# Seven products for the candidate's aggregation side, ScalarE normalisations and a fused last update in a four-layer graph network kernel

## Chip, cores and metric

The kernel runs on one core of a Trainium2 chip. The metric is the device time of one execution in microseconds (us), here the median of three runs. A core has five engines that run side by side, each with its own queue in order: TensorE (PE, matrix products; its weight loads are shown apart as PEld), VectorE (DVE), ScalarE (ACT), GpSimd (POOL), and SyncE (SP), which in this kernel issues nearly all DMAs. Products land in PSUM, eight banks of 128 x 512 f32; everything else lives in SBUF, and data that must change its layout goes through DRAM.

## What is computed

128 graphs of 128 nodes with 256 features pass four layers. Each layer adds its result to its input and normalises over the features:

```
x = layernorm(x + L0(x, adj, a0..a3))          # attention, one score product for each edge kind
x = layernorm(x + L1(x, adj, W_msg, W_upd))    # mean over neighbours
x = layernorm(x + L2(x, adj, weight, w_ih, w_hh, b_ih, b_hh))   # three gated steps
x = layernorm(x + L3(x, adj, W, a))            # attention, elu

# L2, with A = (adj != 0) and h = x; three times:
m    = h @ weight[i];  aggr = A^T m
gi   = aggr @ w_ih.T + b_ih;  gh = h @ w_hh.T + b_hh
r    = sigmoid(i_r + h_r);  z = sigmoid(i_z + h_z)
n    = tanh(i_n + r * h_n)                     # the candidate
h    = (1 - z) * n + z * h
```

All is f32; the neighbour sums of layer 2 are made of three bf16 parts that together hold the f32 value.

## The kernel before

**Tiling.** Four graphs form a group (G = 4, T = 512 nodes), and there are 32 groups (NG). Features lie in KC = 2 blocks of 128. In layer 2 the state is kept turned: two tiles hT of [128 features, 512 nodes]. `turned` and `back` turn a tile by way of DRAM: a 32 x 32 block transpose on DVE, a store, four loads. `turned_quick` does it on PE and is used at the very start and end, where nothing else fills the wait.

**Order.** The program first records every operation of all groups as an `Op` with a due time (`paced` spreads a stage's operations between two times, in units of PERIOD, offset by the group). Then a planner (from line 902 on) walks a model of the five engines: at each point it issues, on the engine that can start first, the ready operation with the earliest due time. The cost functions (lines 244 to 258), LANDING (a DMA's time) and HOP, PE_HOP and SLACK (the step from one engine to another) set when the model holds an operation ready. The outcome is a fixed order for each engine; the chip keeps that order and waits on semaphores. So several groups are always under way at once, in different stages.

**Layer 2, function `step`.** For each of three steps: `aggregate` makes the neighbour sums of both feature blocks (24 bf16 products) and ACT copies them to agT. Every gate needs a product of a 256 x 256 weight block with the 256 x 512 state. `gate` does it with seven products of 128 x 128 by 256 columns in place of eight, on sums and differences of the blocks (`sums` for the data, w_sh and w_sm for the weights). The four output quarters share partial sums: one PSUM bank, `shared`, takes products 1, 6, 7 and 4 one after another, and between them `snapshot` has ACT copy the state of the bank to SBUF. The next product into that bank has to wait for the copy. A second bank, `other`, takes 2, 5 and 3, and DVE adds the two parts. `gate` is used for the hidden side of the candidate (q, seven products), and for r and z (hidden and aggregated side together, fourteen each). The aggregated side of the candidate is made by `direct` (line 667): plain products, two 512-column ones for each of the two blocks, left in PSUM.

```
n1, d1 = candidate(1, direct(w_i, agT, C + 1), t1, q1)
n0, d0 = candidate(0, direct(w_i, agT, C), t0, q0)
```

`candidate` (line 757) forms (r + 1) q on DVE, adds the PSUM sum on DVE, takes tanh on ACT and h - n on POOL. `update` (line 766) makes the new h = n + 0.5 (z + 1)(h - n) on DVE in two instructions, and turns it back to rows (tile hn, through way_h), after which the next step's bf16 parts are split off.

**Between the layers.** Layer 1's result x2 is stored as rows to way_x2, and turned to way_2, from which the first step's h0T is read. Layer 3 (line 811) reads both again: rT from way_2, to which POOL adds hT, and x3 from way_x2, to which DVE adds hn. So rT and x3 hold x2 + h, once turned and once as rows. The products with w3x read rT; the mean is taken out of w3x beforehand, so only 1/sigma (rstd) is needed there.

**Normalisation.** `statistics` makes mean and variance on DVE and the power -1/2 on POOL. `normalise` (line 468) handles even graphs on POOL (on DVE at the start and end, `quick`) and odd graphs on ACT, with nmr = -mean * rstd. There are four normalisations a group.

Of the kernel before, what the change touches and what calls it, by code (L numbers as in the profile page):

```python
# [18 lines left out]
def kernel(  # L19
# [123 lines left out]
    FAST = ("tensor_scalar", "tensor_scalar_add", "tensor_scalar_mul")  # L143

# [10 lines left out]
    class Op:  # L155
        def __init__(self, engine):
            self.engine, self.calls, self.took, self.landing = engine, [], 0.0, 0.0
            self.after, self.bufs, self.waiting = {}, [], 0
            self.ready, self.nominal, self.urgent = 0.0, 0.0, False
            self.waits = self.holds = False  # L160
            self.rush = 0.0

    class Engine:
# [24 lines left out]
        def __getattr__(self, name):  # L188
            def call(*args, **kw):
# [8 lines left out]
                n = 1  # L198
                for v in out + ins:
                    n = max(n, m_of(v))  # L200
                short = self is PE and BF16 in [v.buf.dtype for v in ins]
                op.took += SPLIT if short else self.cost(name, n, "accum_out" in kw)
                op.landing = LANDING if name == "dma_start" else 0.0

                tensors = [v for v in ins if m_of(v) > 4]
                if self is POOL:
                    op.waits, op.holds = True, name == "memset" or len(tensors) > 1
                elif self is DVE and name not in ("transpose", "bn_stats"):
                    op.waits = op.holds = not any(v.buf.pool is psum for v in out + tensors) and (
                        len(tensors) > 1 or (name in FAST and m_of(out[0]) > 4)  # L210
                    )
# [27 lines left out]
    LANDING = 4.2  # L239
    HOP = 0.235  # L240
    PE_HOP = 0.55
    SLACK = 0.873

    def pe_cost(op, n, sums):
        return 0.11 if op == "transpose" else 0.222 if n <= P else 0.003 + n / 599.0

    SPLIT = 0.056

    def dve_cost(op, n, sums):
        return 0.14 + n * (0.00056 if op in FAST else 0.00106)  # L250

    def act_cost(op, n, sums):
        return 0.6 if op == "dma_start" else 0.17 + n * 0.001 + (0.2 if sums else 0.0)

    def pool_cost(op, n, sums):
        return 0.2 + n * 0.00266 if op in FAST else 0.55 if op == "memset" else 1.2 if n < 64 else 0.25 + n * 0.0023
# [5 lines left out]
    SP = Engine("SP", nc.sync, lambda op, n, sums: 0.6)  # L262
# [3 lines left out]
    PERIOD = 82.744  # L266
    SPAN = 2.0
    EAGER, RUSH = 5.34, 0.516
    L0_START, L0_END, L1_START, L1_END, L3_START, L3_END = -2.032, -1.293, -0.75, -0.05, 0.173, 0.919
    H_END, M_START, M_END = 0.179, 0.179, 0.503  # L270

    def paced(start, end, pe_only=False):
# [3 lines left out]
        for op, t in zip(line, took):  # L276
            op.nominal = (start + (end - start) * sofar / total) * PERIOD
            op.urgent = pe_only
            sofar += t
        line.clear()  # L280

# [24 lines left out]
    w_sm = tile_of("w_sm", [P, NL, 3, 2, P])  # L306

    def weights():
# [3 lines left out]
        for src, tag, bufs in ((w_ih, "hT", 6), (w_hh, "rest", 4)):  # L312
# [9 lines left out]
        paced(-2.6, -2.5)  # L322
        for k, a in enumerate((a0, a1, a2, a3)):
            SP.dma_start(out=acol[:, k, :], in_=a.rearrange("(c p) -> p c", p=P))
        paced(-2.2, -2.1)
# [8 lines left out]
        paced(-2.0, -1.5)  # L334
# [22 lines left out]
        for i in range(NL):  # L357
            wT = tile_of("h0T", [P, KC, D], 4)
# [23 lines left out]
        for n in range(NL + 1):  # L382
            by, gates = POOL if n > 1 else DVE, 3 if n == 0 else 2
# [35 lines left out]
        paced(-1.9, -0.2)  # L419


    def turned(src, n, tag):

        way = tile_of(f"way_{tag}", [n, P, P], 8 if tag == "2" else 4, F32, dram)
        for first in range(0, n, G):
            z = tile_of("z", [P, G, P], 4)[:, : min(n, G)]
            DVE.transpose(z, src[:, first : first + G])
            SP.dma_start(out=way[first : first + G].rearrange("n p c -> p n c"), in_=z)
        return way

# [7 lines left out]
    def turned_quick(dst, blocks):  # L438
# [5 lines left out]
        ACT.copy(dst, ps[:, : len(blocks) * P])  # L444
# [10 lines left out]
    def statistics(res, tag):  # L455
# [3 lines left out]
        rstd = tile_of(f"rstd_{tag}", [P, n], 2)  # L459
        for b in range(n):  # L460
# [5 lines left out]
        return mv, rstd  # L466

    def normalise(res, mv, rstd, tag, quick):

        n = res.shape[1]  # L470
        nmr = tile_of(f"nmr_{tag}", [P, n], 2)
        DVE.scalar_tensor_tensor(nmr, mv[:, :, 0], -1.0, rstd, op0=OP.mult, op1=OP.mult)
        for b in range(0, n, 2):
            (DVE if quick else POOL).tensor_scalar(
                res[:, b, :], res[:, b, :], mv[:, b, 0:1], rstd[:, b : b + 1],
                op0=OP.subtract, op1=OP.mult,
            )
        for b in range(1, n, 2):
            ACT.activation(
                res[:, b, :], res[:, b, :], AF.Identity, bias=nmr[:, b : b + 1], scale=rstd[:, b : b + 1]  # L480
            )
# [26 lines left out]
    def loading(g, s):  # L508
# [12 lines left out]
        paced(g - 2.4, g - 2.1)  # L521
        SP.dma_start(out=s.x, in_=x[graphs].rearrange("b n d -> n b d"))
        paced(g - 1.9, g - 1.8)


    def layer0(g, s):
# [51 lines left out]
        normalise(res, *statistics(res, "0"), "0", g == 0)  # L578
# [12 lines left out]
    def layer1(g, s):  # L591
# [32 lines left out]
        normalise(res, *statistics(res, "1"), "1", g == 0)  # L624

        s.way_x2 = tile_of("way_x2", [P, G, D], 4, F32, dram)
        SP.dma_start(out=s.way_x2, in_=res)
        s.hT, s.parts, s.ways = [], [], []
        for c in range(KC):
            t = tile_of("h0T", [P, T], 4)  # L630
# [12 lines left out]
    def gru(g, s):  # L643
# [5 lines left out]
        def step(i, hT, parts):  # L649
# [16 lines left out]

            def direct(w, v, q, ps=None, of=(0, 1), stop=True):

                start = ps is None
                ps = ps or bank("ps" if q >= C else "gate")  # L670
                with PE:
                    for k in of:
                        PE.matmul(
                            ps, w[:, k, q * P : (q + 1) * P], v[k],
                            start=(start and k == of[0]), stop=(stop and k == of[-1]),
                        )
                return ps
# [25 lines left out]
            def gate(tag, q, sources, copied, added, last=None):  # L703
# [14 lines left out]
                def snapshot(quarter):  # L718
                    copied(t[:, quarter], shared[:, :H], quarter // 2)
                    ops[-1].rush = RUSH  # L720
# [36 lines left out]
            def candidate(c, ps, t, q):  # L757
                DVE.scalar_tensor_tensor(t, t, 1.0, q, op0=OP.add, op1=OP.mult)
                DVE.tensor_add(t, t, ps)
# [3 lines left out]
                POOL.tensor_sub(d, hT[c], n)  # L763
                return n, d

            def update(c, z, n, d):

                DVE.scalar_tensor_tensor(d, z, 1.0, d, op0=OP.add, op1=OP.mult)
                new[c] = tile_of("hT", [P, T], 6)
                DVE.scalar_tensor_tensor(new[c], d, 0.5, n, op0=OP.mult, op1=OP.add)  # L770
                turning[c] = tile_of("hn", [P, G, P], 3)
                flat = turning[c].rearrange(FLAT)
                if g == NG - 1 and i == NL - 1:
                    turned_quick(flat, [new[c][:, b * N : (b + 1) * N] for b in range(G)])
                else:
                    back(flat, turned(new[c].rearrange("p (b n) -> p b n", b=G), G, "h"))
                if i < NL - 1:
                    split_up[c] = split(turning[c], DVE)
# [3 lines left out]
            at = g + i * SPAN / NL  # L782
            w_i = c_gi[:, i]
            of_h = sums(POOL, hT, w_hhT, w_sh, hT, "t_h")
            q0, q1 = gate("q", C, (of_h,), hidden, half_more)
            paced(at, at + H_END, True)
            aggregate(0)
            aggregate(1)
            paced(at + M_START - 0.03, at + M_START, True)
            of_m = sums(DVE, agT, w_i, w_sm[:, i], agps, "t_m")  # L790
            t0, t1 = gate("t_r", R, (of_h, of_m), copy, DVE.tensor_add, tanh(R))
            n1, d1 = candidate(1, direct(w_i, agT, C + 1), t1, q1)
            n0, d0 = candidate(0, direct(w_i, agT, C), t0, q0)
# [3 lines left out]
            paced(at + M_START, at + M_END, True)  # L797
# [4 lines left out]
        s.hT, s.hn = hT, hn  # L802
# [233 lines left out]
```

## Time and profile before

| what | value |
|---|---|
| runs | 2762.44, 2764.06, 2764.56 us (median 2764.06) |
| profiled execution, first to last instruction | 2761.8 us |
| DVE, ACT, POOL busy over the span | 2304.1, 1584.2, 1666.2 us |
| products of `direct`: ps<-agT,c_gi, 128x512 | 768 instructions, 592 ns mean |
| ACT copies of 128x256 out of a gate bank | 372 to 374 ns |
| POOL tensor_scalar of `normalise` (xb, xa, xd, xc) | 1757, 1420, 1238, 1233 ns, 62 each |
| ACT of `normalise`, 128x256 | 586 to 595 ns |
| POOL t_d<-hT,t_n, 128x512 | 1295 ns |
| DVE t_r<-t_r,ps, 128x512 | 684 ns, 192 times |
| DMA traffic | 321.88 MB |

The profile is of one execution. A row names what is written and what is read, the shape, and the mean length of one instruction. Each f32 product is two PE instructions, so 768 instructions are 384 products. Instructions of PE overlap in the records (the next starts before the last one's end), so the distance between two starts says what one costs.

### The profile page before, as it was taken

How to read it: one execution, taken by the hardware profiler on the slowest of the kernel's cores; microseconds unless marked ns; L12 is line 12 of the kernel's file. 1: busy time of each engine (PE TensorE's matmuls, PEld its weight loads, DVE VectorE, ACT ScalarE, POOL GpSimd, SP SyncE). 2: the span in 40 equal slices, each digit the busy share in tenths (PEclk: the TensorE clock that was granted, in tenths of full speed). 3: DMA queues.
4: the chain of work that ended last, by engine and by line, in shares of the span. 5: the costliest groups of instructions: out<-in, count | busy, mean ns of one | idle time of the engine just before them, and what ended most of it. 6: DMA issues, size and time to landing. Idle time of an engine off the chain costs nothing.

```text
span 2761.8 us, 44048 instructions
## 1 busy us (share of the span) xinstructions
PE 2702.3 (98%) x13756; PEld 2138.1 (77%) x13756; DVE 2304.1 (83%) x5108; ACT 1584.2 (57%) x3704; POOL 1666.2 (60%) x1606
## 2 busy tenths in 40 slices
PE   8899999999999999999999999999999999999996
PEld 5677787887887887887887887887887887787774
DVE  5787888888888888888888888888888898888875
ACT  4454665555665655665655665655665655665554
POOL 4544666655666655666655666655676655675542
PEclk9999999999999999999999999999999999999996
DMA  5545555555555556555655556655556555545441
GB/s 121 129 90 99 115 126 129 120 109 124 122 125 131 121 108 129 118 124 133 121 107 127 121 121 134 121 110 123 121 121 134 124 109 120 116 110 118 99 88 43
DMA packets 1397130, 321.88 MB, mean 117 GB/s; under 512 B 1142560, under 2 KB 1388448, under 8 KB 1396896
## 3 DMA queue, kind: packets, MB, share of 16 engines
q1 hardware_dynamic: 1394448, 316.69, 53.7%
q10 hardware_dynamic: 2448, 2.36, 0.3%
q8 instruction: 111, 1.82, 0.3%
q14 instruction: 123, 1.01, 0.1%
HBM read 185.74 MB, written 133.15 MB: 115 GB/s over the span
## 4 chain that ended last, share of the span: by engine, by line
PE 94%; DVE 3%; POOL 1%; ACT 1%; DMA 1%; issue 1%; ACTq 0%; POOLq 0%; DVEq 0%; SPq 0%
PE gate L232 52%; PE ps L232 42%; DVE t_r L232 0%; POOL t_h L232 0%; DVE xb L232 0%; DVE st L232 0%; DMA rest<-in_L_gnn_w_hh_dram 0%; DVE z L232 0%; POOL rstd L232 0%; DMA hn<-in_L_gnn_weight_dram 0%; POOL xa L232 0%; DVE xa L232 0%; DVE t_d L232 0%; POOL t_d L232 0%; DVE hT L232 0%
## 5 line engine op out<-in xcount | busy, mean ns | idle before, releaser
L232 ACT ACTIVATE q<-gate,bhn 128x256 f32<-128x256 f32 x384 | 183.0, 477 | 314.4 <-PE gate L232 313.1
L232 PE MATMUL ps<-agT,c_gi 128*128 128x512 f32 x768 | 356.0, 592 | 0.0
L232 PE MATMUL gate<-t_h,w_hhT 128*128 128x256 f32 x1152 | 345.2, 381 | 5.7 <-ACT t_z L232 4.3
L232 PE MATMUL gate<-t_h,w_sh 128*128 128x256 f32 x1152 | 337.1, 383 | 4.2 <-ACT q L232 1.7
L232 POOL TENSOR_TENSOR rstd<-rstd,neg_half 128x4 f32<-128x4 f32 (+1 forms) x128 | 142.4, 1112 | 218.2 <-DVE rstd L232 215.1
L232 PEld LDWEIGHTS gate<-t_h,w_sh 128*128 128x128 f32 x1152 | 213.7, 191 | 62.8 <-issue 30.4
L232 PEld LDWEIGHTS ps<-xs,xT 128*128 128x128 f32 x2048 | 249.7, 193 | 11.5 <-ACT xs L232 2.6
L232 PEld LDWEIGHTS gate<-t_h,w_hhT 128*128 128x128 f32 x1152 | 211.7, 191 | 56.1 <-issue 16.3
L232 PE MATMUL ps<-xs,xT 128*128 128x128 f32 x2048 | 251.8, 276 | 2.2 <-ACT xs L232 1.3
L232 ACT COPY t_z<-gate 128x256 f32<-128x256 f32 x288 | 107.1, 372 | 244.6 <-PE gate L232 244.0
L232 PE MATMUL ps<-w_um,x1T 128*128 128x512 f32 x512 | 237.1, 595 | 0.2 <-ACT x1T L232 0.2
L232 PEld LDWEIGHTS ps<-agT,c_gi 128*128 128x128 f32 x768 | 145.8, 190 | 114.5 <-issue 106.0
L232 PE MATMUL gate<-agT,c_gi 128*128 128x256 f32 x768 | 229.2, 380 | 2.6 <-ACT agT L232 2.6
L232 PE MATMUL gate<-t_m,c_gi 128*128 128x256 f32 x768 | 228.5, 379 | 0.0
L232 PE MATMUL gate<-t_m,w_sm 128*128 128x256 f32 x768 | 228.4, 379 | 0.0
L232 PE MATMUL gate<-hT,w_hhT 128*128 128x256 f32 x768 | 222.8, 385 | 5.6 <-DVE hT L232 5.6
L232 POOL TENSOR_SCALAR mk<-a_f 128x512 uint8<-128x512 f32 x128 | 201.3, 1579 | 12.2 <-DVE alpha L232 6.6
L232 ACT ACTIVATE xs<-xT,acol 128x512 f32<-128x512 f32 x256 | 182.1, 717 | 40.9 <-PE ps L232 31.5
L232 POOL MEMSET hu<- 128x1 f32 x128 | 10.3, 96 | 303.8 <-DVE fac L232 224.5
L232 DVE TENSOR_TENSOR t_z<-gate,t_z 128x256 f32<-128x256 f32 x192 | 104.2, 543 | 101.4 <-ACT t_z L232 53.7
L232 POOL TENSOR_TENSOR t_d<-h0T,t_n 128x512 f32<-128x512 f32 x64 | 82.9, 1295 | 174.0 <-ACT t_n L232 171.1
L232 PEld LDWEIGHTS gate<-hT,w_hhT 128*128 128x128 f32 x768 | 141.8, 191 | 48.1 <-issue 23.6
(197 smaller groups left out, 7280.1 us busy)
## 6 DMA issues: line engine op xcount, KB each, us to landing
way_h<-z SPq DMA_DIRECT2D x190, 256.0 KB, 2.4
hn<-way_h SPq DMA_DIRECT2D x760, 64.0 KB, 2.4
way<-z SPq DMA_DIRECT2D x126, 256.0 KB, 3.2
x_blocks<-in_x_dram SPq DMA_DIRECT2D x256, 64.0 KB, 2.3
x_in<-in_x_dram SPq DMA_DIRECT2D x32, 512.0 KB, 3.8
way_x<-xb SPq DMA_DIRECT2D x32, 512.0 KB, 2.9
way_p<-z SPq DMA_DIRECT2D x62, 256.0 KB, 2.6
probT<-way_p SPq DMA_DIRECT2D x248, 64.0 KB, 2.3
```

The lines of the kernel that those rows point to most:

```text
L232: getattr(self.engine, name)(*[a.real() if isinstance(a, View) else a for a in args], **{k: a.real() if isinstance(a, View) else a for k, ...
```

## The change

**Candidate.** The aggregated side of the candidate becomes a `gate` of its own (t_i, source of_m alone), with seven products of 256 columns; `direct` is gone. Its extra weights make w_sm three gates wide. The sum now lies in SBUF, and POOL adds it (DVE in the last group).

**Normalisation.** `normalise` runs on ACT alone, apart from even graphs where `quick` holds. `shift` takes the place of nmr.

**Last step.** The turned x2 is loaded into rT at the head of the last step. POOL adds n onto it, and `update` adds 0.5 (z + 1)(h - n) onto that, so that its result is x2 + h, the turned input of layer 3. It is turned through way_3 straight into x3. The store to way_x2, its load, and the adds onto rT and x3 in layer 3 go. h0T and hT share one set of nine buffers.

**Planner.** Costs, DMA times and hops are given anew and in more kinds, due times are given in microseconds by stage, and the first and last six groups have shifts of their own (HEAD, TAIL).

```diff
-            by, gates = POOL if n > 1 else DVE, 3 if n == 0 else 2
+            by, gates = POOL if n > 1 else DVE, 3
...
+        DVE.scalar_tensor_tensor(shift, mv[:, :, 0], -1.0, rstd, op0=OP.mult, op1=OP.mult)
+        return shift, rstd
+
+    def normalise(res, shift, rstd, quick):
+
+        for b in range(res.shape[1]):
+            if quick and b % 2 == 0:
+                DVE.tensor_scalar(
+                    res[:, b, :], res[:, b, :], rstd[:, b : b + 1], shift[:, b : b + 1],
+                    op0=OP.mult, op1=OP.add,
+                )
+            else:
+                ACT.activation(
+                    res[:, b, :], res[:, b, :], AF.Identity, bias=shift[:, b : b + 1], scale=rstd[:, b : b + 1]
+                )
...
-        s.way_x2 = tile_of("way_x2", [P, G, D], 4, F32, dram)
-        SP.dma_start(out=s.way_x2, in_=res)
...
-            t = tile_of("h0T", [P, T], 4)
+            t = tile_of("hT", [P, T], 9)
...
-            def candidate(c, ps, t, q):
+            def candidate(c, aggregated, t, q):
                 DVE.scalar_tensor_tensor(t, t, 1.0, q, op0=OP.add, op1=OP.mult)
-                DVE.tensor_add(t, t, ps)
+                (DVE if g == NG - 1 else POOL).tensor_add(t, t, aggregated)
...
                 POOL.tensor_sub(d, hT[c], n)
+                if last_step:
+                    POOL.tensor_add(s.rT[c], s.rT[c], n)
+                    n = s.rT[c]
                 return n, d
...
                 DVE.scalar_tensor_tensor(d, z, 1.0, d, op0=OP.add, op1=OP.mult)
-                new[c] = tile_of("hT", [P, T], 6)
+                new[c] = n if last_step else tile_of("hT", [P, T], 9)
                 DVE.scalar_tensor_tensor(new[c], d, 0.5, n, op0=OP.mult, op1=OP.add)
...
+                if last_step:
+                    turning[c] = s.x3[:, :, c * P : (c + 1) * P]
                 else:
-                    back(flat, turned(new[c].rearrange("p (b n) -> p b n", b=G), G, "h"))
-                if i < NL - 1:
+                    turning[c] = tile_of("hn", [P, G, P], 3)
+                if last_step and g == NG - 1:
+                    turned_quick(turning[c], [new[c][:, b * N : (b + 1) * N] for b in range(G)])
+                elif last_step:
+                    turn(s.way_x3[:, c], new[c].rearrange("p (b n) -> p b n", [P, G, N], b=G))
+                    if c == 0:
+                        back(
+                            s.x3.rearrange("p b d -> p (b d)"),
+                            s.way_x3.rearrange("b c p n -> (b c) p n", [G * KC, P, P]),
+                        )
...
+            last_step = i == NL - 1
+            if last_step:
+                s.rT = [tile_of("rT", [P, T], 2) for _ in range(KC)]
+                for c in range(KC):
+                    back(s.rT[c], s.ways[c])
+                s.x3 = tile_of("xc", [P, G, D])
+                s.way_x3 = tile_of("way_3", [G, KC, P, P], 4, F32, dram)
...
-            n1, d1 = candidate(1, direct(w_i, agT, C + 1), t1, q1)
-            n0, d0 = candidate(0, direct(w_i, agT, C), t0, q0)
+            i0, i1 = gate("t_i", C, (of_m,), copy, DVE.tensor_add)
+            n1, d1 = candidate(1, i1, t1, q1)
+            n0, d0 = candidate(0, i0, t0, q0)
...
-        rT = []
-        for c in range(KC):
-            t = tile("rT", [P, n * N], 2)
-            cols = slice(first * N, last * N)
-            back(t, s.ways[c][first:last])
-            (DVE if end else POOL).tensor_add(t, t, s.hT[c][:, cols])
-            rT.append(t)
-        x3 = tile("xc", [P, n, D])
-        SP.dma_start(out=x3, in_=s.way_x2[:, first:last])
-        for c in range(KC):
-            cols = slice(c * P, (c + 1) * P)
-            DVE.tensor_add(x3[:, :, cols], x3[:, :, cols], s.hn[c][:, first:last])
-        mv, rstd = statistics(x3, two)
+        x3 = s.x3 if n == G else s.x3[:, first:last]
+        shift, rstd = statistics(x3, two)
```

The planner's part, cut to its core:

```diff
-    LANDING = 4.2
-    HOP = 0.235
-    PE_HOP = 0.55
-    SLACK = 0.873
+    LANDING = {"e": 5.66, "adj_in": 4.0, "x_in": 3.85, "x1T": 3.53, "way_1": 3.2, "way_2": 3.0, "xc": 3.6, "way_f": 2.0}
...
+        if len(ins) - pointers > 1:
+            return 0.22 + n * 0.0021, 0.2 + n * 0.0021
...
-    PERIOD = 82.744
-    SPAN = 2.0
-    EAGER, RUSH = 5.34, 0.516
-    L0_START, L0_END, L1_START, L1_END, L3_START, L3_END = -2.032, -1.293, -0.75, -0.05, 0.173, 0.919
-    H_END, M_START, M_END = 0.179, 0.179, 0.503
+    PERIOD = 81.83483
+    EAGER, RUSH = 5.2365, 0.7497
+    HOP, PE_HOP, SLACK, DMA_SLACK = 0.0946, 0.0838, 0.2615, 1.3152
+    TIMES = {
+        "layer0": ((-168.5025, -107.0697),),
...
+        "step2": ((107.5318, 125.3405), (123.0192, 128.3402), (118.3669, 151.8864),),
+        "layer3": ((179.8537, 241.5793),),
+    }
...
+        at = g * PERIOD
+        if g < len(HEAD):
+            at += HEAD[g][STAGES.index(stage)]
+        elif g >= NG - len(TAIL):
+            at += TAIL[g - NG][STAGES.index(stage)]
+        spread(at + start, at + end, stage[:4] == "step")
```

## The prediction

> **What bounds the kernel now.** I read the page from the top: engines, slices, chain.
>
> ```profile
> span 2761.8 us, 44048 instructions
> PE 2702.3 (98%) x13756; PEld 2138.1 (77%) x13756; DVE 2304.1 (83%) x5108; ACT 1584.2 (57%) x3704; POOL 1666.2 (60%) x1606
> PE   8899999999999999999999999999999999999996
> PEclk9999999999999999999999999999999999999996
> PE 94%; DVE 3%; POOL 1%; ACT 1%; DMA 1%; issue 1%; ACTq 0%; POOLq 0%; DVEq 0%; SPq 0%
> ```
>
> TensorE is busy in every slice but the first two and the last, at full granted clock, and carries 94% of the chain that ends last. Busy time alone could hide slack, so I asked for stretches:
>
> ```profile
> 0.00:60.00 60.00, 47.60 (x249) 34.68 (x250) 31.57 (x77) 25.86 (x58) 25.56 (x33) 1.00 0.60 124
> 383.00:1200.00 817.00, 817.00 (x4225) 652.94 (x4224) 705.98 (x1566) 483.88 (x1134) 514.47 (x493) 1.00 0.57 121
> 2650.00:2700.00 50.00, 43.91 (x187) 32.25 (x185) 32.90 (x68) 25.76 (x62) 24.00 (x23) 0.92 0.40 87
> 2730.00:2762.00 32.00, 12.13 (x36) 7.48 (x34) 15.53 (x51) 16.94 (x44) 8.88 (x9) 0.60 0.12 42
> ```
>
> (columns: length, then PE, weight load, DVE, ACT, POOL busy, clock, DMA share, GB/s). From 383 to 1200 us PE has no idle time. All its idle time, 2761.8 - 2702.3 = 59.5 us, lies at the two ends. The chain in order of time gives the period, one candidate product group per period:
>
> ```profile
> 377.31 3.43 PE ps L232 x8
> 459.98 3.43 PE ps L232 x8
> 542.65 3.43 PE ps L232 x8
> ```
>
> 82.67 us for each group of four graphs. The timeline of PE shows what one product costs, by distance from start to start:
>
> ```profile
> 1203.86 3.60 PE L232 MATMUL ps<-agT,c_gi 128*128 128x512 f32 x8
> 1207.29 0.59 PE L232 MATMUL gate<-hT,w_hhT 128*128 128x256 f32 x2
> 1207.72 0.59 PE L232 MATMUL gate<-agT,c_gi 128*128 128x256 f32 x2
> 1208.15 0.59 PE L232 MATMUL gate<-t_h,w_hhT 128*128 128x256 f32 x2
> ```
>
> Eight instructions (four products of 512 columns) take 1207.29 - 1203.86 = 3.43 us; a product of 256 columns takes 0.431 us (1203.86 - 1202.13 over four). Check: a period holds 105 gate products (45.3 us), 3 candidate groups (10.3), 72 bf16 products with their edges (about 4.4), and layers 0, 1 and 3 (7.2 + 1.7 + 6.9 + 1.7 + 3.5 + 1.7 = 22.7): 82.7 us, the period. So the middle is PE work laid end to end, with nothing lost; only fewer PE columns, or the ends, can shorten it.
>
> **What the Trainium skill says.** "Perfetto Trace Analysis", Identifying the Most-Contended Engine, warns that matmul busy time is no measure of the distance to peak. The trace agrees: instructions of 0.38 us each start 0.216 us apart, hence my distances. "TensorE: Matmul & The Clock Gate", Back-to-back issue gap, gives about N/2.4 + 2.5 ns; the bf16 products here, 0.057 us apart at N=128, fit, and each half of an f32 product at N=256, 0.216 us, costs what the page has for 512 columns. Products cost by their columns, so one product of eight less is a gain in full. "PSUM — Partial Sum Buffer", The four PSUM rules, says that GpSimd cannot reach PSUM; no POOL row here has a PSUM operand, and so the add that moves to POOL needs its sum evicted first. "SBUF — State Buffer", Who interferes with whom: a DVE instruction with two SBUF inputs and a POOL instruction that reads SBUF block each other. The trace fits: DVE's t_d<-t_z,t_d takes 920 ns against 689 for xd<-ps,xd of the same size.
>
> **The change part by part.**
>
> *Seven products (t_i).* Before, each step does 4 products of 512 columns, 3.43 us. After, 7 of 256: 7 x 0.431 = 3.02. Gain 0.414 us a step, on the path; 32 groups x 3 steps = 96 steps: **-39.7 us**. In counts +576 matmul instructions. The weight loads (0.19 us, two to a product) stay under the products, as they do for r and z.
>
> *What t_i adds elsewhere.* ACT: 4 copies of 128x256 at 0.373 = 1.49 us a step. DVE: one add of 256 (0.409) and one of 512 (0.690) = 1.10 a step; against it t_r<-t_r,ps goes, 2 x 0.684. POOL takes that add, 2 x 1.29 us (row t_d<-hT,t_n, 1295 ns, same shape). The extra combined weights of the set-up are three small POOL operations made wider, some 0.3 us each, under the first loads.
>
> *Normalisations.* POOL loses 8 tensor_scalar a group: 2 x (1.757 + 1.420 + 1.238 + 1.233) = 11.3 us; ACT gains 8 x 0.59 = 4.7. The nmr product stays under the name shift. The two POOL and two ACT halves ran side by side (2.4 to 3.5 us for the POOL pair), four on ACT take 2.3: no longer.
>
> *Last update.* Each group loses the write and read of way_x2 (1 MB of traffic), two DVE adds onto x3 (0.72 each) and the two POOL adds rT + hT (1.278), and gains two POOL adds of n. Eight loads hn<-way_h of 64 KB become four of 128 KB; SP issues six DMAs fewer (0.47 us each). The eight rT loads move from layer 3 to the head of the last step, on SP ahead of that step's other loads: 8 x 0.47 = 3.8 us of issue, in the 20 us to spare named below. On POOL the second d stands behind the first rT add, 1.28 us later, under the z gate's products (6 us of PE). x3's one buffer is now filled after the last step and freed by layer 3's add, a stage later; nothing.
>
> Sums per period: DVE 71.4 (705.98 x 82.67/817) - 4.1 + 3.3 - 1.4 = 69.2 of 81.4, 85%; ACT 49.0 + 4.5 + 4.7 = 58.2, 71% where it was 59%; POOL 52.1 - 11.3 + 7.7 = 48.5, 60%. None becomes the bound. I cost them at nothing in the middle: PE's 81.4 us cover them. If that cover is gone, the price is a PE stall, below.
>
> *Step latency.* The candidate now goes through the gate's evictions and a POOL add 0.6 us longer than DVE's. A step nearly alone takes 2689.8 to 2724.8 = 35 us, while a period gives each step 55: 20 us to spare. Nothing.
>
> *The tail.* The last group's w3x products begin at 2727.70, after hT (2726.05 + 0.69) and two rT adds of 0.42. Those go; so does the 0.42 add onto x3 after the last copy. I take **-1.5 us**, from 0 to -3; the new POOL adds (d, rT, d, rT, 1.28 each from 2720.1) end at 2725.2, just before the second update at 2726.05.
>
> *New due times and costs.* The order at the ends changes, with shifts for each of the first and last six groups. The trace cannot price an order. Bounds: half of the 59.5 us of idle PE won back (-30), or some handshakes late (+10). The new costs are nearer to the rows (512-wide POOL add 1.295 against 1.295 measured, before 1.43; DMA to landing per tensor, 2.0 to 5.66, where the DMA view shows 2.0 to 5.7 and the old figure was 4.2 for all). I take **-2** for the ends and **+2** for stalls in the middle.
>
> *The wait that the change adds.* A gate's shared bank takes products 1, 6, 7, 4 with an ACT snapshot between them, and PE is in order: a late snapshot stops everything behind. Three such handshakes a step are new. An exposed one is seen at the end:
>
> ```profile
> 2657.79 0.59 PE L232 MATMUL gate<-t_m,w_sm 128*128 128x256 f32 x2
> 2658.85 0.70 PE L232 MATMUL gate<-t_h,w_sh 128*128 128x256 f32 x2 [0.46 <-ACT t_z L232]
> ```
>
> 1.06 us from start to start in place of 0.43: 0.63 us lost. In the middle the nine per step that exist now lose nothing, because other groups' products stand between.
>
> Sum: 2761.8 - 39.7 - 1.5 - 2 + 2 = 2720.6 of span; some 2.3 us separate the span from the median of 2764.06 (runs 2762.44 to 2764.56), so 2723; I say 2722.
>
> **Rivals.** *Partly eaten (0.13).* ACT at 71%, or SP held by a load, bares some handshakes: rT's two buffers are now held from the last step to the w3x products, most of a period, and a load that waits for them holds every DMA behind it on SP. Half of the gain lost: 2764 - 20 = 2744. For it: the candidate's 3.43 us of filler that needed no handshake are gone. Against: 23 us of layer products and the other step remain as filler.
>
> *Slower (0.08).* At ACT's queue, one new handshake a step is exposed throughout: 96 x 0.63 = 60 us against 40 won, 2784. It decides from 0.414/0.63 = 0.66 exposed handshakes a step. Against it: zero PE idle in 817 us with nine of them.
>
> *Ends won back (0.10).* A third of the idle PE time goes: 2722 - 20 = 2702. For it: the ends are chains of small waits, which order can mend; against: the last 32 us are one group's dependent chain.
>
> *No effect (0.01)*: products of the same columns as before; the code shows 7 x 256 for 4 x 512.
>
> **Numbers.** The likeliest, 0.68, 2722, own range 2708 to 2735. Range 2701 to 2744: it takes in half of the ends' rival and half of the partial one. Faster by over 0.2% (5.5 us, about what a measurement of this kernel can tell from no change) 0.89: the likeliest, the ends, and nearly all of the partial case; within it 0.03; slower 0.08.
>
> **What would show it.** Period 82.67 - 1.24 = 81.43 and no PE idle in the middle; matmuls near 14330; ACT near 70%, POOL near 57% of the span; no row ps<-agT,c_gi. If PE waits for ACT t_i in the middle, the handshake was mispriced; if PE is full and the period is longer than 81.43, the products are; if only the idle time of the ends differs, the order is.

## The result and the profile after

| | before | after | predicted |
|---|---|---|---|
| median of the runs | 2764.06 us | 2755.27 us (2750.87 to 2756.05, five runs) | 2722 (2701 to 2744) |
| span of the profiled execution | 2761.8 us | 2749.0 us | 2720.6 |
| matmul instructions | 13756 | 14332 | near 14330 |

The ratio is 0.9963, with a 95% interval of 0.9952 to 0.9975: faster, but by 9 us where 42 were predicted. The time lies outside the range. The profiled execution is the fastest of the five (2750.87 us), so the profile shows 12.8 us of gain where the medians show 8.8.

The page of the changed kernel begins like this (span, busy time of each engine, PE's busy tenths in 40 slices):

```profile
span 2749.0 us, 45121 instructions
PE 2678.5 (97%) x14332; PEld 2232.4 (81%) x14332; DVE 2183.6 (79%) x5044; ACT 1807.6 (66%) x4336; POOL 1570.5 (57%) x1546
PE   8999999999999999999999999999999999999995
```

The counts of products are as worked out, POOL's share too, and ACT is at 66% for the 70% expected. The page alone shows nothing wrong: the slices round 98% and 100% to the same 9. The windows (length, then PE, weight load, DVE, ACT, POOL busy, clock, DMA share, GB/s) do:

```profile
383.00:1200.00 817.00, 807.82 (x4359) 677.27 (x4358) 655.27 (x1532) 549.46 (x1322) 474.59 (x468) 1.00 0.53 108
1200.00:1600.00 400.00, 399.86 (x2165) 338.40 (x2165) 327.80 (x769) 272.81 (x658) 233.46 (x233) 1.00 0.54 110
1600.00:2000.00 400.00, 399.93 (x2178) 339.17 (x2178) 325.36 (x757) 275.55 (x664) 236.90 (x235) 1.00 0.54 109
2000.00:2400.00 400.00, 395.28 (x2127) 330.07 (x2126) 327.98 (x748) 269.62 (x646) 242.04 (x233) 1.00 0.52 107
```

From 1200 to 2000 us TensorE is as full as it was; from 383 to 1200 it now idles 9.2 us, where it idled 0.0. DVE is *less* busy there than before (655 against 706 us), so no engine has become the bound. The list of what PE waited for between 383 and 2400 us (in total, times, longest) was empty before. Now it begins:

```profile
PE gate L228 <- ACT t_z L228: 4.4, 8, 1.5
PE gate L228 <- DVE t_r L228: 2.3, 3, 1.2
PE ps L228 <- DVE rest L228: 2.0, 1, 2.0
PE gate L228 <- DVE q L228: 1.6, 2, 1.3
```

Many short stalls with several names, and t_i hardly among them (DVE t_i 0.2 us, once). Idle time understates them, since products overlap in the records. So I added up, over all PE instructions, the distance from start to start less what such an instruction costs in a full stretch (0.057 us in bf16, 0.216 for half an f32 product of 256 columns, 0.429 of 512). This is TensorE's loss, by where it lies:

| loss, us | 0 to 300 | 300 to 1100 | 1100 to 2000 | 2000 to 2500 | to the end | sum | products |
|---|---|---|---|---|---|---|---|
| before | 32.6 | 4.1 | 4.6 | 2.5 | 47.3 | 91.1 | 2656.0 |
| after | 29.6 | 26.0 | 6.3 | 16.9 | 37.1 | 115.8 | 2616.4 |

The products, counted at these costs, take 39.6 us less, as predicted (39.7). The two ends give 13.2 (79.9 to 66.7). The stretch between takes 38.0 back (11.2 to 49.2). What lies outside TensorE's own work, before its first product and after its last, grew by 2.1 us (14.7 to 16.8): 39.6 + 13.2 - 38.0 - 2.1 is the 12.8 us of the profiled executions, to a tenth.

### The profile page after: what moved, and what is told of

It reads as the page before. It is cut to its first block, busy times and chain, and to the rows that moved or that the text cites. A ratio compares the mean times of both kernels' runs of the same rounds, so it can differ in the third digit from the quotient of the medians.

```text
span 2749.0 us, 45121 instructions
## 1 busy us (share of the span) xinstructions
PE 2678.5 (97%) x14332; PEld 2232.4 (81%) x14332; DVE 2183.6 (79%) x5044; ACT 1807.6 (66%) x4336; POOL 1570.5 (57%) x1546
## 5 line engine op out<-in xcount | busy, mean ns | idle before, releaser
L228 POOL TENSOR_TENSOR t_r<-t_r,t_i 128x512 f32<-128x512 f32 x186 | 244.4, 1324 | 280.8 <-ACT t_i L228 207.5
L228 PE MATMUL gate<-t_m,w_sm 128*128 128x256 f32 x1152 | 341.5, 380 | 1.0 <-DVE t_m L228 0.5
L228 PE MATMUL gate<-agT,c_gi 128*128 128x256 f32 x1152 | 340.3, 380 | 1.6 <-ACT t_z L228 0.6
L228 PE MATMUL gate<-t_m,c_gi 128*128 128x256 f32 x1152 | 340.4, 379 | 0.0
L228 PE MATMUL gate<-hT,w_hhT 128*128 128x256 f32 x1152 | 331.1, 382 | 3.9 <-ACT t_z L228 2.0
L228 POOL TENSOR_TENSOR t_d<-hT,t_n 128x512 f32<-128x512 f32 x192 | 250.8, 1319 | 45.1 <-ACT t_n L228 44.5
L228 PEld LDWEIGHTS gate<-t_m,c_gi 128*128 128x128 f32 x1152 | 218.3, 190 | 39.3 <-issue 10.0
L228 PEld LDWEIGHTS gate<-agT,c_gi 128*128 128x128 f32 x1152 | 217.4, 190 | 34.4 <-ACT t_z L228 1.8
L228 PEld LDWEIGHTS gate<-t_m,w_sm 128*128 128x128 f32 x1152 | 217.7, 190 | 33.1 <-ACT t_i L228 1.7
L228 ACT COPY t_i<-gate 128x256 f32<-128x256 f32 x384 | 142.3, 371 | 110.1 <-PE gate L228 105.1
```

Of the source, the lines that this page charges most:

```text
L228: getattr(self.engine, name)(*[a.real() if isinstance(a, View) else a for a in args], **{k: a.real() if isinstance(a, View) else a for k, ...
```

## What waits for what in one stall

Engine by engine, the timeline of one stall near 790 us (start, length, engine, operation, tiles, idle time before and its releaser), some other instructions left out:

```profile
789.07 0.91 DVE L228 SCALAR_TENSOR_TENSOR rT<-t_d,rT 128x512 f32<-128x512 f32 x1
...
790.30 1.26 POOL L228 TENSOR_TENSOR xd<-xd,xc 128x512 f32<-128x512 f32 x1
790.65 0.93 DVE L228 SCALAR_TENSOR_TENSOR shift<-mv,rstd 128x4 f32<-128x4 f32 x1
...
791.50 0.41 DVE L228 SCALAR_TENSOR_TENSOR q<-gate,q 128x256 f32<-128x256 f32 x1
791.61 0.60 ACT L228 ACTIVATE xb<-xb,shift,rstd 128x256 f32<-128x256 f32 x1 [1.30 <-DVE shift L228]
...
791.97 0.48 PE L228 MATMUL gate<-hT,w_sh 128*128 128x256 f32 x1 [1.30 <-DVE q L228]
```

shift has four numbers a partition and takes 0.93 us. It ends when GpSimd's addition ends (791.58 and 791.56 us). Behind it stands q, and TensorE waits for q: 1.30 us. ScalarE waits for shift, and stands still for 1.30 us too. How often that happens is in the tile views (shortest, median, longest in ns); first nmr of before, then of after shift, rstd and the reciprocal rinv:

```profile
L232 DVE SCALAR_TENSOR_TENSOR nmr<-mv,rstd x128: 122/152/1219, 49.9 to 2757.9; 128x4 f32<-128x4 f32 x126, 128x2 f32<-128x2 f32 x2
```

```profile
L228 DVE SCALAR_TENSOR_TENSOR shift<-mv,rstd x128: 114/326/1241, 52.1 to 2744.2; 128x4 f32<-128x4 f32 x126, 128x2 f32<-128x2 f32 x2
```

```profile
L228 DVE TENSOR_SCALAR rstd<-mv x128: 131/170/1243, 50.8 to 2743.2; 128x4 f32<-128x4 f32 x126, 128x2 f32<-128x2 f32 x2
```

```profile
L228 DVE RECIPROCAL rinv<-rsum x64: 133/170/194, 42.4 to 2732.7; 128x4 f32<-128x4 f32 x63, 128x2 f32<-128x2 f32 x1
```

Over 600 ns were 3 of 128 nmr before and 36 of 128 shift after; of rstd, 3 before and 27 after. What GpSimd does next to it has changed. Before, the power was followed on GpSimd by the even graphs' normalisation, which reads one tensor; nmr ran beside it at 0.15 to 0.36 us in nearly all records. The change took the normalisations off GpSimd, and an addition or subtraction of two tensors now mostly follows the power: 35 of the 36 long shifts ran beside one. "SBUF — State Buffer", Who interferes with whom, in the Trainium skill, says that a DVE instruction with two SBUF inputs contends with a GpSimd instruction that reads SBUF for a shared port pair, and calls that pair an exclusive lock. shift agrees, small as it is. For rstd, a tensor_scalar, the page has this only in a two-port form; no run here shows which form it took, but it was lengthened alike. The reciprocal rinv is not lengthened in this run.

The second half is reserve. For each product that needs the work of another engine, a reckoning on the trace (the kernel's own dependences, with the recorded starts and ends) gives how long the last thing it needs had been done when it started:

| 383 to 1100 us | such products a period | done under 0.6 us ahead | a tenth has less than | median |
|---|---|---|---|---|
| before | 94 | 3.0 | 0.91 us | 2.95 us |
| after | 108 | 22.1 | 0.29 us | 1.66 us |

A delay of 1.1 us is mostly covered in the first order and often exposed in the second. But it is not exposed everywhere. From 1100 to 2000 us the reserve is as thin (22.1 under 0.6 us), and 22 of 88 shift and rstd last over 600 ns there, against 15 of 74 from 300 to 1100 us; yet only 6.3 us are lost. In that stretch the order repeats from group to group: the first product of layer 1 (ps<-w_um,x1T) follows that of the group before by 81.5 to 82.0 us, eleven times in a row. From 300 to 1100 us this distance is anything from 64 to 96 us. In the kernel before it is 82.67 us 25 times in a row, through the whole middle. So in this kernel the loss lies where the order changes from group to group. Repetition by itself is no cover, as e1 and e5 below show; what a long shift costs depends on what happens to stand behind it.

## The experiments

"In its order" means that the order which the planner found for a kernel is written out as a list, and the instructions are issued by that list, so that an edit moves nothing else. Times are medians, with the ratio to the kernel before. "Middle" is the stretch from 300 to 2500 us, where the changed kernel loses 49.2 us. The expectations name theories by letters: S the shifts of the due times, M the planner's smaller margins, H the handshakes of the new gate on a fuller ScalarE, O an order (due times) that does not fit, and later L, small VectorE instructions held up by GpSimd, and A, ScalarE's fuller queue. L came up after e5.

**The planner's parts.**

e1_noshift, the changed kernel with `HEAD = TAIL = ((0.0,) * 7,) * 6`.

> The changed kernel with all shifts of the first and last six groups set to zero, so that every group has the same due times; all else as changed. Theory S (the shifts): the PE losses of the changed kernel outside its ends (26 us from 300 to 1100 us, 17 us from 2000 to 2500 us, 6 us between) come from the order that the shifts give those groups; without them 300 to 1100 and 2000 to 2500 lose under 8 us together, the ends may lose up to 13 us more, and the time is 2725 to 2742. Theory M (the margins: the planner's model now allows only 0.08 to 0.26 us from one engine to the next where it allowed 0.24 to 0.87): slack is as thin as before, the middle still loses over 25 us, time 2750 to 2765. Theory H (the new gate's handshakes on a fuller ScalarE): unchanged, about 2755.

2766.41 us, 1.0010 (1.0001 to 1.0019). The loss moves about (33.8 us from 300 to 1100, 9.5 from 2000 to 2500) and the ends lose 13 us more. The shifts help; the stalls are not theirs. From 375 to 1050 us the groups now follow one another by 84.6 to 84.8 us, later by 81.5: an order that repeats can stall in every period. The time is just above the range of theory M.

e2_margin, the old margins with the new due times.

```diff
-    HOP, PE_HOP, SLACK, DMA_SLACK = 0.0946, 0.0838, 0.2615, 1.3152
+    HOP, PE_HOP, SLACK, DMA_SLACK = 0.235, 0.55, 0.873, 1.3152
```

> The changed kernel with the planner's three hops set back to their old values (0.235, 0.55 and 0.873 us), shifts kept. Theory M: the order gains slack, the losses in the middle go, 2722 to 2735. Theory S: the losses from 300 to 1100 and from 2000 to 2500 us stay, within 10 us of the changed kernel, 2745 to 2765. Theory H: about 2755 too.

2813.05, 1.0178 (1.0163 to 1.0193), slower than any of the theories had it. With these due times, larger margins make a worse order.

**The seven products.** e3_direct puts the four products of 512 columns and DVE's addition from PSUM back into the changed kernel; e4_seven puts only the seven products and GpSimd's addition into the kernel before, with two st buffers for four, to find room.

```diff
-            i0, i1 = gate("t_i", C, (of_m,), copy, DVE.tensor_add)
-            n1, d1 = candidate(1, i1, t1, q1)
+            n1, d1 = candidate(1, direct(w_i, agT, C + 1), t1, q1)
```

> The changed kernel with the candidate's aggregated side back as four products of 512 columns left in PSUM and added by DVE; planner, shifts, normalisation and last update as changed. PE work rises by 39.7 us. Theory H: the losses in the middle fall to those of the kernel before (under 10 us), so it costs only 5 to 15 us over the changed kernel: 2760 to 2770. Theories S and M: the losses stay and the PE work comes on top: 2785 to 2800.

> The kernel before with the seven products and the POOL add alone (statistics' small tile has two buffers in place of four, for room); old planner, old hops, no shifts, old normalisation, old last update. Theories S and M: the old order's slack covers the new gate, the period is 81.43 us and the time 2722 to 2730. Theory H: PE waits for the new gate's copies in every step; the time is 2740 to 2765.

2825.10, 1.0227 (1.0210 to 1.0244), and 2881.92, 1.0427 (1.0411 to 1.0442). No expected range was met. Each operation set is bad in the other's due times: stalls with other names (ACT t_z 32.6 us in the first, DVE t_z and ACT t_z 37 in the second). Neither tells what the products cost by themselves, but the first shows that the planner's new numbers are no gain without the seven products.

e7_double, in its order, makes the three snapshot copies of t_i twice: 288 ScalarE copies, 107 us, all at the added wait.

```diff
+                        if tag == "t_i":
+                            copied(t[:, quarter], shared[:, :H], quarter // 2)
```

> The changed kernel in its very own order of instructions on every engine, with each of the three intermediate copies of the new gate (t_i) made twice on ScalarE: 288 copies of 0.37 us more, 107 us of ScalarE work, and each of the new gate's handshakes 0.37 us longer. Theory H: these handshakes bound PE, and the time rises by 40 to 110 us. Theory O: the new gate's own copies have cover in this order, and the time rises by less than 15 us.

2775.58, 1.0044 (1.0029 to 1.0059): 20 us over the changed kernel, between the two expected ranges. PE waited for ACT t_i 1.4 us from 383 to 2400 us. If a second copy costs at least as much as the first, which stands first in line for the reserve, the copies did not cost the missing 33 us; that step is argued, not shown.

**Other due times.** e5_replan_a and e6_replan_b: due times for the changed operations chosen anew on the planner's model (PERIOD 81.09 and shifts near zero in the first; near the given ones in the second).

> The changed kernel, every operation of it kept; only the planner's due times, hops and shifts are other numbers (period 81.09, shifts near zero). They were chosen so that each engine's fixed order, replayed with the durations that the changed kernel's trace shows, leaves TensorE fewest gaps. Theory O (the order: what PE loses is set by how well the due times fit the operations as they are, whatever the operations): from 300 to 2500 us the loss falls from 49 us to under 20 and the time is 2710 to 2732. Theory H (the seven products' copies on ScalarE cost PE time as such): no order takes it away; 2745 to 2760.

> As the run before, with due times that stay near the changed kernel's own and keep its shifts. Theory O: part of the loss goes, 2725 to 2745. Theory H: 2745 to 2760.

2784.51, 1.0081 (1.0066 to 1.0096), and 2821.52, 1.0204 (1.0185 to 1.0223). The hope for a better order fell. But e5 lays the mechanism bare. What PE waited for from 383 to 2400 us is nearly all one name (34.9 of 38.2 us):

```profile
PE gate L228 <- DVE q L228: 34.9, 22, 2.8
```

and its timeline shows the same scene as above; the wait comes 22 times, about once in a period of 83.67 us:

```profile
1216.59 2.63 POOL L228 TENSOR_TENSOR xd<-xd,xc 128x512 f32<-128x512 f32 x2
...
1216.80 1.22 DVE L228 SCALAR_TENSOR_TENSOR shift<-mv,rstd 128x4 f32<-128x4 f32 x1
...
1218.56 0.38 DVE L228 SCALAR_TENSOR_TENSOR q<-gate,q 128x256 f32<-128x256 f32 x1
...
1219.00 0.70 PE L228 MATMUL gate<-hT,w_sh 128*128 128x256 f32 x2 [1.44 <-DVE q L228]
```

The planner's model counts only tensors of more than four elements as holding the port, so it cannot see this; nor could the model of the kernel before.

**The normalisations, in the order of before.** e8_before_norm moves only the even graphs' normalisation to ScalarE.

> The kernel before in its very own order, with one part of the change alone: the even graphs' normalisation on ScalarE in the place where POOL had it. ScalarE gains 4 operations of 0.59 us a normalisation's pair less what it had, 4.7 us a group (6% of the period), in an order that loses nothing in the middle. Prediction's reading (covered, costs nothing): 2755 to 2768, middle loss under 10 us. Theory H2 (a fuller ScalarE bares handshakes): 2775 to 2800.

2774.38, 1.0037 (1.0022 to 1.0051), 6 us above the prediction's reading. The middle is untouched, 4.1, 4.6 and 2.6 us, although nmr now takes over 600 ns in 31 of 128 records (before: 3):

```profile
L232 DVE SCALAR_TENSOR_TENSOR nmr<-mv,rstd x128: 121/153/1230, 51.5 to 2770.0; 128x4 f32<-128x4 f32 x126, 128x2 f32<-128x2 f32 x2
```

```profile
383.00:1200.00 817.00, 817.00 (x4200) 651.68 (x4200) 711.01 (x1564) 518.24 (x1212) 406.77 (x415) 1.00 0.57 122
```

So this lengthening alone costs nothing in that order. It is milder than that of the change: rstd stays short, and all nmr together rose from 27 to 36 us, where shift and rstd of the changed kernel take 107. The two ends lose 12.3 us more (39.5 and 52.7). The likeliest reading is that four normalisations on one engine do take longer there than two on each of two; nothing else was edited.

**Taking the lengthening away, in the order of after.** e9_copy1 and e10_copy2 replace GpSimd's addition by one or two copies (665 ns each in the mean, for 1324 of the addition), and so leave the hidden side out of the candidate.

```diff
-                (DVE if g == NG - 1 else POOL).tensor_add(t, t, aggregated)
+                if g == NG - 1:
+                    DVE.tensor_add(t, t, aggregated)
+                else:
+                    with POOL:
+                        POOL.tensor_copy(t, aggregated)
```

> The changed kernel with every instruction in the place that its planner gave it, but the 186 GpSimd additions of the products onto t_r are copies of the products (t_r<-t_i, one operand in SBUF instead of two): the gate's other half is left out of the candidate. Theory L (the lost 38 us in 300 to 2500 us come from small VectorE instructions that a GpSimd instruction with two SBUF operands holds up): shift and rstd keep their 0.15 us next to these copies, TensorE's loss in that stretch falls from 49 us to under 35, span under 2738. Theory O (the order as such does not fit the chip's latencies, whatever GpSimd reads): only the 0.4 us by which a copy is shorter counts, loss 44 to 50, span 2744 to 2750.

> As the run before, but the copy is made twice, so that GpSimd's part lasts longer than the addition did (about 1.8 us against 1.32) and still reads one SBUF operand at a time. L: the loss in 300 to 2500 us still falls, under 42 us, span under 2745, although t_r is later. O: t_r is 0.5 us later, the loss grows, 50 to 65 us, span 2750 to 2770.

2742.59, 0.9922 (0.9907 to 0.9937), and 2745.43, 0.9933 (0.9918 to 0.9948): 12.7 and 9.8 us below the changed kernel. The second keeps GpSimd as long as the addition did, so most of the gain is the missing second operand. Theory L is not met in full: the loss in the middle fell less than it expected (to 38.9 and 43.4), and both spans are longer (2741.0 and 2747.3 us). The second run's profile is the slowest of its runs (2742.8 to 2749.5).

e13_recip replaces the two small instructions by one-operand ones, and leaves out the sum with EPS and the product with the mean.

```diff
-        DVE.tensor_scalar_add(rstd, mv[:, :, 1], EPS)
+        DVE.reciprocal(rstd, mv[:, :, 1])
...
-        DVE.scalar_tensor_tensor(shift, mv[:, :, 0], -1.0, rstd, op0=OP.mult, op1=OP.mult)
+        DVE.reciprocal(shift, rstd)
```

> The changed kernel with every instruction in its place, but the two small VectorE instructions of each normalisation read one operand and are of a kind that was never lengthened in the trace (RECIPROCAL 128x4: 133 to 194 ns in 63 records, against 114 to 1241 ns for shift and 131 to 1243 ns for rstd). The sum with EPS and the product with the mean are left out; what waits for what is the same. Theory L (VectorE's small instructions held up by GpSimd are what PE meets): moving the trace's own delays forward with shift and rstd at their short time takes 13 us off, so 2738 to 2746 us. Theory A (ScalarE's fuller queue is what PE meets): 2751 to 2759.

2740.15, 0.9907 (0.9893 to 0.9922): 15.1 us below the changed kernel, as expected of L. (The profiled executions are 10.2 us apart, 2749.0 and 2738.8 us: one is the fastest of its runs, the other the slowest.) The tile view of shift, the window in which 9.2 us were idle, and what is left of the wait for ACT t_z, which was 4.4 us:

```profile
L228 DVE RECIPROCAL shift<-rstd x128: 133/168/180, 52.1 to 2734.0; 128x4 f32<-128x4 f32 x126, 128x2 f32<-128x2 f32 x2
```

```profile
383.00:1200.00 817.00, 812.01 (x4399) 683.06 (x4398) 648.69 (x1547) 554.39 (x1335) 483.40 (x474) 1.00 0.53 109
```

```profile
PE gate L228 <- ACT t_z L228: 0.8, 2, 0.5
```

Same order and same waits; only these operands differ. 0.2 to 0.3 us on average came off each of 252 instructions that together last 106 us in the changed kernel.

e16_no_even leaves out 248 ScalarE instructions, those that the change brought there; ScalarE's busy time falls by 105 us (1807.6 to 1703.0).

> The changed kernel in its order, but the normalisation of graphs 0 and 2 of each four (groups 1 to 31), which the change moved to ScalarE, is left out: ScalarE has 248 instructions, about 130 us, less. A: the loss in 300 to 2500 us (49 us) falls by more than 20, 2725 to 2738 us. L: by the same reckoning 6 us, 2745 to 2752.

2754.34, 0.9964 (0.9952 to 0.9977): 0.9 us below the changed kernel, and 16 above the top of A's range. Theory A falls. L's range (2745 to 2752) is missed too, by 2 us.

e17_recip_copy has the edits of e9 and e13 together.

> The changed kernel in its order with both edits of e9 and e13: copies of t_i in the place of GpSimd's additions, and one-operand instructions in the place of shift and rstd (so the gate's other half, the sum with EPS and the product with the mean are left out). If the lengthened VectorE instructions are what the prediction missed, the two add up: 2755 - 12.7 - 15.1 = 2727, 2722 to 2734, near the 2722 predicted. If they take away the same delays, 2736 to 2741.

2735.23, 0.9895 (0.9881 to 0.9910): 20.0 us below the changed kernel. The two overlap in part. Its losses are 27.1, 17.0, 4.4, 13.9, 36.8: in the middle 35.3 us, where the kernel before loses 11.2 and the changed kernel 49.2. So most of the middle's loss outlasts both edits.

**Cures that leave nothing out.** e11_shift_pool has shift made by two GpSimd products in shift's place; e12_replan_shift does so in the order of e5. e14_behind makes them in the power's own group; e15_allpool moves the sum with EPS there too. e18_add_dve gives the addition of t_i back to DVE.

```diff
         with POOL:
             POOL.tensor_tensor(rstd, rstd, neg_half[:, :n], OP.pow)
+            POOL.tensor_tensor(shift, mv[:, :, 0], neg_one[:, :n], OP.mult)
+            POOL.tensor_tensor(shift, shift, rstd, OP.mult)
```

> The changed kernel with every instruction in its place, but shift (minus mean times rstd, 128x4) is worked out by two tiny GpSimd instructions right behind the power instead of one VectorE instruction. L: VectorE never stands still up to 1.2 us for shift, the stalls behind it go, loss in 300 to 2500 us 49 to about 35 to 43, span 2735 to 2745; GpSimd's two instructions (1 to 2 us for each of 126) may give part back. O: no fall, 49 or more, span 2749 to 2760.

> The order of e5_replan_a (2784.5 us, one stall of 1.6 us in each group's period, behind a shift that took 1.22 us) with every instruction in its place, and shift on GpSimd as in the run before. L: the stall of each period goes, some 26 to 32 times 1.6 us: 2784 to 2735 to 2750 us, period 83.7 to about 82. O: the stall is a matter of the order, it stays: 2780 to 2790.

> The changed kernel in its order, but shift is worked out in GpSimd's own group right behind the power (two products of 128x4, about 0.28 us each), with no GpSimd work between, and no VectorE instruction for it. L: the lengthened shift goes (8 us by the same reckoning), GpSimd's next work is 0.6 us later: 2742 to 2752. A: 2753 to 2765.

> As the run before, and the sum with EPS too is GpSimd's, so that VectorE has no small instruction with two operands or in its fast form left in a normalisation. L: 2736 to 2750. A: 2753 to 2770.

> The changed kernel in its order with one part undone: the addition of t_i onto t_r is VectorE's again in every group (about 0.69 us of VectorE for 1.32 us of GpSimd, 186 times), with the right result. L: fewer GpSimd instructions with two SBUF operands, so t_d, rT, rest, shift and rstd are lengthened less, the candidate is 0.6 us earlier, but VectorE has 4.1 us more in each group's period: 2740 to 2757. If it is VectorE's load that PE meets: 2760 to 2780.

| run | median | ratio (95%) |
|---|---|---|
| e11_shift_pool | 2771.30 | 1.0024 (1.0016 to 1.0032) |
| e12_replan_shift | 2768.97 | 1.0018 (1.0012 to 1.0025) |
| e14_behind | 2754.18 | 0.9962 (0.9947 to 0.9977) |
| e15_allpool | 2758.73 | 0.9979 (0.9971 to 0.9988) |
| e18_add_dve | 2776.35 | 1.0046 (1.0030 to 1.0063) |

In e12 the wait behind shift shrank from 34.9 us to this (same view, the same window), and 15.5 us were won on e5:

```profile
PE gate L228 <- DVE q L228: 8.3, 21, 1.5
PE gate L228 <- ACT t_z L228: 3.9, 21, 0.5
```

That is less than the 35 to 50 expected: something else was late next, ScalarE's t_z among it. All four others went against L's numbers; e14 and e15 fell into A's ranges, though e16 leaves A no ground. In e11 shift stands in GpSimd's queue, and PE's waits for ACT t_z stay (5.4 us); in e18 DVE has 30 us more from 383 to 1200 us (685 against 655), and its time lies where VectorE's load was expected to put it. e14 equals the changed kernel: PE now waits 1.9 us for POOL t_h, which was not in its list, so that what shift no longer costs seems to go into GpSimd's queue. No cure beats the changed kernel by more than the noise.

## Why the prediction was wrong

By its own steps:

- *Seven products*, -39.7 us: right, by the mechanism forecast. From 1100 to 2000 us the groups follow one another by 81.5 us in most cases, where 81.43 was forecast and 82.67 was before.
- *Stalls in the middle*, +2: this is the term that failed. They took 38.0 us. The largest part of it that the runs show was put at nothing:
- *"The nmr product stays under the name shift"*, costed at nothing: the step that failed. The instruction stayed, its neighbour on GpSimd did not. The prediction named the port rule and applied it to t_d alone, a long instruction; it should have been asked of every small instruction too that the moved work leaves beside GpSimd's additions. e13 puts 15 us on shift and rstd.
- *GpSimd takes that add*, covered: not free either. e9 and e10 put 10 to 13 us on its second operand, and e17 20 on both together.
- *Sums per period*, none becomes the bound: right, and beside the point. "PE's 81.4 us cover them" did not follow from it: a queue at 80% in fixed order can still be late.
- *Normalisations*, "no longer": wrong at the ends (12.3 us in e8), right in the middle.
- *The ends*, -2, with -1.5 for the tail: the loss there fell by 13.2. That this gain, 10 us more than forecast, brought the total nearer to the prediction is luck.
- *The bound of +10* for late handshakes came from no row. The reserve of each handshake, which the trace of before could have given for the old order, was not asked for.
- *The added wait*: the rivals' mechanism (ScalarE's t_i snapshots, ACT at 71%) is not borne out. PE waits 0.2 us for t_i in the middle, and leaving 248 instructions off ScalarE changes nothing (e16); e7 leaves room for some microseconds.

Of the 33 us between 2722 and 2755, runs account for at most 20 (e17); some 3 of these may be GpSimd's shorter part, by which e9 and e10 differ. The other 13 are open, and so is most of what the profile shows: with both edits the middle still loses 24 us more than before. Longer t_d or rest will not do as the cause by themselves, since both were longer in the kernel before, where the middle lost nothing by it (rest<-rest 1073 ns before, 796 after):

```profile
L232 DVE SCALAR_TENSOR_TENSOR t_d<-t_z,t_d 128x512 f32<-128x512 f32 x192 | 174.4, 920 | 3.0 <-ACT t_z L232 3.0
L228 DVE SCALAR_TENSOR_TENSOR t_d<-t_z,t_d 128x512 f32<-128x512 f32 x192 | 154.2, 805 | 28.5 <-ACT t_z L228 27.4 <-ACT q L228 0.3 <-ACT t_r L228 0.2
```

What stays is the order: its reserve is thin, and what stands behind a late instruction differs from one stretch to the next. No run isolated this. The nearest to it are e8, which loses nothing in the middle with 31 long nmr, in the old order with its reserve, and the stretch of 1100 to 2000 us, which loses 6.3 us with thin reserve. An order for the new operations that keeps its reserve was not found.

## What to carry to other kernels

When work leaves an engine, look at what now runs there in its place, and at who shares a port with it; a moved instruction's cost is also its old neighbours' cost. In a fixed order on in-order queues, how full the engines are is not the measure: ask of the trace how long before each TensorE instruction its last input was ready, and hold that against the longest delay that any instruction in the queue suffered. An order with small margins can pay for a delay that its model leaves out, and what it pays depends on what stands behind: long shifts cost next to nothing from 1100 to 2000 us of the changed kernel, and a stall in nearly every period of e5.

## What the runs showed of the hardware

- A VectorE instruction of 128x4 lasts 0.15 us or up to 1.24 us, by what GpSimd does beside it: nearly as long as a whole addition of 128x512 (1.32 us).
- In the places of shift and rstd, RECIPROCAL of 128x4 stays within 180 ns (e13). It is not always untouched: one of 64 rinv in the kernel before took 537 ns, beside GpSimd's mk, and two of 128 reciprocals of 128x1 (fac) after took 449 and 522 ns, beside mk too. All three ended 24 to 25 ns after mk.
- Beside a GpSimd instruction that reads one tensor, the normalisation of before, nmr mostly took 0.15 or 0.35 us, at most 0.42. Beside mk alone, which also reads one tensor, shift took up to 0.58 us. Beside instructions on two tensors it took up to 1.24.
- nmr could be held and still end while GpSimd's instruction went on: of the 28 beside the normalisation of xb, 26 took 350 to 358 ns and ended 0.66 us before it.
- Beside a GpSimd memset, which reads nothing, 14 shifts took 165 ns at most.
- A GpSimd copy of 128x512 takes 0.67 us, half of the addition's 1.32.
- A stall of TensorE costs more than its idle time: in the start-to-start distances after 361.05 us of the changed kernel, one that shows a gap of 0.745 us loses 0.91, and the product behind it 0.10 more.
